# Neighbour aggregation by seven block products, with an earlier start of some group steps, in a graph and GRU layer

## The chip, the core and the metric

The kernel runs on one core of a Trainium2 chip. The metric is the device time in microseconds (us) of one execution; the time of a kernel is the median over its executions. Five engines work in parallel on the core: TensorE (PE in the profile; its weight loads are PEld), VectorE (DVE), ScalarE (ACT), GpSimd (POOL) and SyncE (SP, which here issues DMA transfers). Each takes its own instructions in order and waits on semaphores of the others.

## What is computed

There are B = 32 batches of N = 512 nodes with D = 256 features, all in float32. A layer norm and a relu come first; the layer has a convolution branch (a 1x1 convolution, then one of 17 taps), a neighbour aggregation and a GRU gate:

```python
h = jnp.maximum(_layernorm(x, axis=-1), 0.0)
# on h:
s = x @ w_se.T + b_se                                # 3 values per node
sq = jnp.sum(s * s, axis=-1)
dist = sq[:, :, None] + sq[:, None, :] - 2.0 * jnp.einsum('bnd,bmd->bnm', s, s)
A = jnp.exp(-dist) * mask                            # mask: a symmetric 0/1 adjacency
msg = jax.nn.relu(x @ w_msg.T + b_msg)
x_nmp = jnp.einsum('bnm,bmd->bnd', A, msg)           # the aggregation
x_in = jnp.concatenate([x_conv, x_nmp], axis=-1)
gi = x_in @ w_ih.T + b_ih
gh = x @ w_hh.T + b_hh
# r, z: sigmoids of the sums; n = tanh(gi_n + r * gh_n)
return (1.0 - z) * nn_ + z * x
```

The output is the input x plus the result of the layer.

## The kernel before

The batches are worked in two groups of 16 (GB). Each group has two stages, and one stage for all batches in pairs comes last.

`first_part(g)` makes the normalised rows (`statistics` L281, `normalise` L293), transposes them (`transpose_h` L307, hT, which is also written to memory), runs the 1x1 convolution (`conv1`) and takes the windows to a spectrum (`windows_to_freq`). The order in it is written by hand, in `manual_schedule`. Group one also builds the spectrum of the 17 taps there, and loads the weights of its first three spectrum products (`load_unit`, L911).

`nodes(g)` (L920) does two things side by side. One is the spectrum products (`product` L372, PSUM tile `py`, three products of two matmuls of 256 columns each): 36 units over the 16 batches in group one, so two or three in each iteration, and 40 units over the first 13 batches in group two, three each and four in the last, so that the last three iterations have none. POOL prepares a product (`both` L369 and L370, `wsum` L356), ACT and DVE take its result out (`y` L396 to L398). The other is the neighbour part, per batch:

- `load_h`, `by_chunks` (ACT copies, L422) bring hT in the order wanted.
- `message` (L425): eight matmuls of 259 columns into `pm` (256 of the message and 3 of s), the bias added by DVE (L438, L439), relu by ACT (L440).
- `features` (L442): five small DVE operations; `factors` (L452): transposes on PE into `psl`, `psr`, copied out by ACT.
- `affinity` (L464): four matmuls into `pd` (distances), the exponential on ACT into a tile `e` (L474), the transposed adjacency by DVE (`at`, L476), and the product of both by DVE (L477): the tile `A`.
- `aggregate` (L480): two times four matmuls of 128x128 by 512 columns into `pn` (L485), copied by ACT to `nmp` (L487), which `save_nmp` writes to memory.

The loop (L937 to L960) is staggered: iteration i makes the factors and affinity of batch i+1, the messages and features of batch i+2 (`begin(i + 2)`), and the aggregation of batch i, with products between. A scheduler may move instructions in `nodes`; a float32 matmul is two records in the profile[...].

The last stage (L992) works with pairs of batches. Its gates are matrix products on 2x2 blocks by seven products each, whose sums POOL makes in advance (`sums` L566). Before the first gates, POOL's queue issues the loads of the first pair (`load_pair(0, nc.gpsimd)`, L536 to L547: `hp`, `yt`, `np`) and of the gate weights (`load_combined` L532, `sw`); `inverse` (L572, PSUM tile pc) turns the spectrum back.

## Time and profile before

| what | us |
|---|---|
| median of 12 executions | 1847.69 |
| lowest and highest of them | 1844.35, 1853.54 |
| the profiled execution | 1846.12 |
| its span in the profile | 1844.3 |
| PE busy in the span | 1822.1 |
| DVE busy | 1102.9 |
| ACT busy | 582.6 |
| POOL busy | 589.0 |

By the timeline, `first_part(0)` runs to 166, `nodes(0)` to about 452, `first_part(1)` to 577, `nodes(1)` to 878.4, and the gates from there to the end. In a profile line, an entry such as L485 is a line of the kernel, `pn<-A,msg` says what is written from what, x512 counts instructions, and after the bar come busy time, the mean of one in ns, and the idle time just before with what ended it. In the chain of waits every line is start, length, engine, tile, line and count, in order of time; a stretch in which only PE stands there is one in which nothing but PE's own work sets the end.

### The profile page before, as it was taken

To read this page: it belongs to the slowest core of one execution; us is meant where nothing else is said; L and a number is where in the kernel's file an instruction comes from. 1 tells how busy PE (TensorE), PEld (TensorE's weight loads), DVE (VectorE), ACT (ScalarE), POOL (GpSimd) and SP (SyncE) were. 2 spreads that over 40 slices of the span, in tenths; PEclk is the share of its full clock that TensorE was granted. 3 is DMA by queue.
4 is the path that set the end of the run, shared out by engine and by line. 5 is a ranking of instruction groups with operands and counts; after the bars stand their busy time and mean duration, and the time that the engine had idled before them with its cause. 6 is when DMAs were issued, how large, how long until landed. Compare 5 with 4: busy or idle time off the path is not lost.

```text
span 1844.3 us, 20105 instructions
## 1 busy us (share of the span) xinstructions
PE 1822.1 (99%) x6610; PEld 1086.8 (59%) x6610; DVE 1102.9 (60%) x2221; ACT 582.6 (32%) x1082; POOL 589.0 (32%) x572
## 2 busy tenths in 40 slices
PE   9999999999999999999999999999999999999998
PEld 6777666666898676675545554555455544555443
DVE  7775655554885555545266456655666466645666
ACT  3545443432345334333222221222122221222121
POOL 3331333334432344445321323133222323133221
PEclk9999999999999999999999999999999999999999
DMA  9999898775578987777422443234422442244412
GB/s 230 301 277 240 238 253 240 192 208 182 187 245 207 245 246 234 219 205 258 116 86 36 118 120 107 57 77 120 120 83 38 120 120 91 48 101 120 112 25 52
DMA packets 307452, 289.26 MB, mean 157 GB/s; under 512 B 148028, under 2 KB 237148, under 8 KB 306964
## 3 DMA queue, kind: packets, MB, share of 16 engines
q1 hardware_dynamic: 281300, 224.22, 46.1%
q10 hardware_dynamic: 19024, 38.68, 5.8%
q0 software_dynamic: 7024, 25.07, 4.9%
q8 instruction: 53, 0.87, 0.2%
q14 instruction: 51, 0.42, 0.1%
HBM read 191.50 MB, written 96.40 MB: 156 GB/s over the span
## 4 chain that ended last, share of the span: by engine, by line
PE 90%; DVE 3%; issue 2%; POOL 2%; DMA 2%; ACT 1%; SPq 0%; POOLq 0%; ACTq 0%; DVEq 0%
PE pg L592 29%; PE pn L592 14%; PE pn L485 12%; PE py L390 11%; PE pm L436 6%; PE pc L580 5%; PE pc L325 3%; PE px L340 3%; PE pw L256 2%; PE pd L471 2%; PE phT L312 1%; DMA w<-in_w_ihT_dram 1%; PE psr L460 1%; DVE xn L304 1%; DVE stats L285 1%
## 5 line engine op out<-in xcount | busy, mean ns | idle before, releaser
L485 PE MATMUL pn<-A,msg 128*128 128x512 f32 x512 | 225.0, 592 | 0.0
L592 PE MATMUL pg<-hp,sw 128*128 128x512 f32 x434 | 221.8, 593 | 0.7 <-DVE rz L611 0.5
L592 PE MATMUL pg<-cp,sw 128*128 128x512 f32 x434 | 221.6, 592 | 0.0
L592 PE MATMUL pg<-np,sw 128*128 128x512 f32 x434 | 221.6, 592 | 0.0
L570 POOL TENSOR_TENSOR hp<-hp 128x512 f32<-128x512 f32 x64 | 81.0, 1276 | 412.2 <-DMA hp<-hd 293.2
L369 POOL TENSOR_TENSOR both<-xf 128x256 f32<-128x256 f32 x78 | 60.7, 778 | 325.1 <-PE py L390 293.9
L485 PEld LDWEIGHTS pn<-A,msg 128*128 128x128 f32 x512 | 97.1, 190 | 110.6 <-issue 107.7
L570 POOL TENSOR_TENSOR cp<-cp 128x512 f32<-128x512 f32 x64 | 80.5, 1269 | 233.5 <-ACT cp L586 232.2
L390 PE MATMUL py<-wt,both 128*128 128x256 f32 x624 | 150.4, 384 | 0.7 <-issue 0.7
L607 ACT ACTIVATE rz<-rz,brz 128x512 f32<-128x512 f32 x93 | 67.2, 724 | 260.0 <-DVE rz L611 260.0
L397 DVE TENSOR_TENSOR y<-y,py 128x256 f32<-128x256 f32 x78 | 31.9, 409 | 190.7 <-ACT y L396 190.7
L592 PEld LDWEIGHTS pg<-hp,sw 128*128 128x128 f32 x434 | 82.2, 190 | 104.8 <-issue 98.1
L592 PEld LDWEIGHTS pg<-np,sw 128*128 128x128 f32 x434 | 82.5, 190 | 103.8 <-issue 103.8
L592 PEld LDWEIGHTS pg<-cp,sw 128*128 128x128 f32 x434 | 82.5, 190 | 103.8 <-issue 103.8
L390 PEld LDWEIGHTS py<-wt,both 128*128 128x128 f32 x624 | 114.1, 190 | 42.9 <-issue 29.1
L477 DVE TENSOR_TENSOR A<-e,at 128x512 f32<-128x512 f32 x128 | 111.9, 912 | 36.5 <-ACT e L474 36.2
L356 POOL TENSOR_TENSOR wsum<-wt 128x512 f32<-128x512 f32 x78 | 108.2, 1388 | 49.6 <-DMA wt<-wd 39.2
L730 ACT ACTIVATE nt<-nt,vech 128x512 f32<-128x512 f32 x64 | 46.4, 725 | 235.4 <-DVE nt L729 235.4
L325 PE MATMUL pc<-w,hT 128*128 128x256 f32 x512 | 118.2, 384 | 2.0 <-DVE hT L313 2.0
L436 PE MATMUL pm<-wmsg,hq 128*128 128x259 f32 x512 | 117.6, 382 | 1.0 <-ACT hq L422 1.0
L592 PE MATMUL pn<-np,sw 128*128 128x512 f32 x224 | 114.4, 592 | 0.0
L592 PE MATMUL pn<-cp,sw 128*128 128x512 f32 x224 | 114.4, 592 | 0.0
(145 smaller groups left out, 2956.7 us busy)
## 6 DMA issues: line engine op xcount, KB each, us to landing
wt<-wd SPq DMA_DIRECT2D x160, 256.0 KB, 4.2
adj<-in_adj_dram SPq DMA_DIRECT2D x128, 256.0 KB, 5.7
wd<-wst SPq DMA_DIRECT2D x64, 320.0 KB, 5.0
yd<-y ACTq DMA_DIRECT2D x80, 256.0 KB, 4.2
yt<-yd SPq DMA_DIRECT2D x30, 640.0 KB, 7.4
hd<-hT SPq DMA_DIRECT2D x32, 512.0 KB, 4.3
nd<-nmp ACTq DMA_DIRECT2D x32, 512.0 KB, 4.2
xb<-in_x_dram SPq DMA_DIRECT2D x128, 128.0 KB, 3.8
```

Of the source, the lines that this page charges most:

```text
L325: nc.tensor.matmul(p[:, j, :], HT[b][:, ic, c * P : (c + 1) * P], w1[:, ic, :], start=(ic == 0), stop=(ic == DC - 1))
L340: nc.tensor.matmul(p[:, j * 2 * L : (j + 1) * 2 * L], H1[b][:, c0 + j, ic * P : (ic + 1) * P], fwd, start=True, stop=True)
L356: nc.gpsimd.tensor_tensor(t, WT[g, u][:, 0], WT[g, u][:, 1], op=ALU.add)
L369: nc.gpsimd.tensor_tensor(both[:, 0], re, im, op=ALU.add)
L390: nc.tensor.matmul(dst, v[:, ic, :], w[:, ic, :], start=(ic == 0), stop=(ic == DC - 1))
L436: nc.tensor.matmul(p[:, : D + NS], hq[:, ic, c * P : (c + 1) * P], wmsg[:, ic, :], start=(ic == 0), stop=(ic == DC - 1))
L477: nc.vector.tensor_mul(A[b][:, mc, :], e, at)
L485: nc.tensor.matmul(p, MSG[b][:, mc, dc * P : (dc + 1) * P], A[b][:, mc, :], start=(mc == 0), stop=(mc == NC - 1))
L570: nc.gpsimd.tensor_tensor(t[:, dst, :], t[:, a, :], t[:, b, :], op=sub)
L580: nc.tensor.matmul(bk[:, t0:t1], YT[p][j][:, c, oc * P : (oc + 1) * P], back[:, n : n + t1 - t0], start=(c == 0), stop=(c == len(spans) - ...
L592: nc.tensor.matmul(bk[:, t], sw[:, k, q, o, :], terms[k][q][:, t], start=(first and i == 0), stop=(i == len(ks) - 1), skip_group_check=True)
L607: nc.scalar.activation(rz[:, g, j, :], src, AF.Sigmoid, bias=brz[:, g : g + 1], scale=1.0)
```

## The change

The aggregation is computed by seven products on 2x2 blocks instead of eight matmuls of 512 columns. Per batch, message blocks are summed by DVE (`message_sums`, four operations of 128x256), affinity blocks by POOL (`affinity_sums`, four of 128x512), and seven block products of two matmuls of 256 columns each go into three PSUM tiles, b1 to b3, of which the same half is used. The results come out by two ACT copies and five DVE adds. `aggregate` is now a generator with three parts, two blocks, then three, then two; the affinity of the next batch lies between the first and the second part, a product between the second and the third. The exponential is written straight into `A`, the tile `e` is gone, and `at` and `sr` have one buffer instead of two.

Besides: at the start of each group the order is by hand, and the two halves of the second batch's message lie before and after the first factors; in group two the statistics of the third batch come ahead of the second's normalise, and its normalise ahead of the second's transposes; hT of batch 0 is half made on ACT; `load_h` is one batch further ahead and comes behind `begin`; and the weights of the first three products are loaded behind `first_part(0)`.

```diff
@@ transpose_h
-            nc.vector.tensor_scalar(HT[b][:, dc, :], p, 0.0, None, op0=ALU.max)
+            if b == 0 and dc > 0:
+                nc.scalar.activation(HT[b][:, dc, :], p, AF.Relu)
+            else:
+                nc.vector.tensor_scalar(HT[b][:, dc, :], p, 0.0, None, op0=ALU.max)
@@ message
-    def message(b):
+    def message(b, halves=range(2)):
...
-        for c0 in range(0, NC, h):
+        for c0 in (h * k for k in halves):
@@ factors
-        t = SR[b] = pools["nodes"].tile([P, N], FP, tag="sr", name=f"sr_{b}", bufs=2)
+        t = SR[b] = pools["nodes"].tile([P, N], FP, tag="sr", name=f"sr_{b}", bufs=1)
@@ affinity
-            e = pools["nodes"].tile([P, N], FP, tag="e", name=f"e_{b}_{mc}", bufs=2)
-            nc.scalar.activation(e, pd[mc], AF.Exp)
-            at = pools["nodes"].tile([P, N], FP, tag="at", name=f"at_{b}_{mc}", bufs=2)
+            nc.scalar.activation(A[b][:, mc, :], pd[mc], AF.Exp)
+            at = pools["nodes"].tile([P, N], FP, tag="at", name=f"at_{b}_{mc}", bufs=1)
             nc.vector.transpose(at.rearrange("p (j k) -> p j k", k=32), ADJ[b][:, :, 32 * mc : 32 * (mc + 1)])
-            nc.vector.tensor_mul(A[b][:, mc, :], e, at)
+            nc.vector.tensor_mul(A[b][:, mc, :], A[b][:, mc, :], at)
@@ new
+    def message_sums(b):
+        m = MSG[b].rearrange("p (k c) (i d) -> p i k c d", k=2, i=DC)
+        (a11, a12), (a21, a22) = (m[:, 0, 0], m[:, 0, 1]), (m[:, 1, 0], m[:, 1, 1])
+        t = SM[b] = pools["nodes"].tile([P, 3, H2, P], FP, tag="sm", name=f"sm_{b}", bufs=1)
+        s1, s2, s4 = (t[:, k] for k in range(3))
+        nc.vector.tensor_add(s1, a21, a22)
+        nc.vector.tensor_sub(s2, s1, a11)
+        nc.vector.tensor_sub(a21, a11, a21)
+        nc.vector.tensor_sub(s4, a12, s2)
+
+    def affinity_sums(b):
+        m = A[b].rearrange("p (k c) (j n) -> p k j c n", k=2, j=2)
+        (b11, b12), (b21, b22) = (m[:, 0, 0], m[:, 0, 1]), (m[:, 1, 0], m[:, 1, 1])
+        t = TA[b] = pools["nodes"].tile([P, 3, H2, N // 2], FP, tag="ta", name=f"ta_{b}", bufs=1)
+        t1, t2, t4 = (t[:, k] for k in range(3))
+        sub = ALU.subtract
+        nc.gpsimd.tensor_tensor(t1, b12, b11, op=sub)
+        nc.gpsimd.tensor_tensor(t2, b22, t1, op=sub)
+        nc.gpsimd.tensor_tensor(b12, b22, b12, op=sub)
+        nc.gpsimd.tensor_tensor(t4, b21, t2, op=sub)
@@ aggregate
-        for dc in range(DC):
-            p = bank(f"pn_{b}_{dc}")
-            for mc in range(NC):
-                nc.tensor.matmul(p, MSG[b][:, mc, dc * P : (dc + 1) * P], A[b][:, mc, :],
-                                 start=(mc == 0), stop=(mc == NC - 1))
-            nc.scalar.copy(NMP[b][:, dc, :], p)
+        def into(bk, w, v, first):
+            for c in range(H2):
+                nc.tensor.matmul(bk[:, lo], w[:, c], v[:, c], start=(first and c == 0), stop=(c == H2 - 1), skip_group_check=True)
+
+        b1, b2, b3 = (bank(f"pn{k}_{b}") for k in range(3))
+
+        p1, u2, u3 = out[:, 1, lo], out[:, 0, hi], out[:, 1, hi]
+        into(b1, m[:, 0, 0], a[:, 0, 0], True)
+        nc.scalar.copy(p1, b1[:, lo])
+        into(b2, s2, t2, True)
+        nc.vector.tensor_add(u2, p1, b2[:, lo])
+        yield
+        into(b1, m[:, 0, 1], a[:, 1, 0], False)
+        nc.scalar.copy(out[:, 0, lo], b1[:, lo])
+        into(b2, m[:, 1, 0], a[:, 0, 1], False)
+        nc.vector.tensor_add(u3, p1, b2[:, lo])
+        into(b3, s1, t1, True)
+        nc.vector.tensor_add(out[:, 1, hi], u3, b3[:, lo])
+        yield
+        into(b2, m[:, 1, 1], t4, False)
+        nc.vector.tensor_add(out[:, 1, lo], p1, b2[:, lo])
+        into(b3, s4, a[:, 1, 1], False)
+        nc.vector.tensor_add(out[:, 0, hi], u2, b3[:, lo])
+        yield
@@ first_part
         statistics(b0 + 1)
+        if g > 0:
+            statistics(b0 + 2)
         normalise(b0 + 1, g > 0)
...
-                transpose_h(b + 1)
-                statistics(b + 2)
-                normalise(b + 2)
+                if g == 0:
+                    transpose_h(b + 1)
+                    statistics(b + 2)
+                    normalise(b + 2)
+                else:
+                    normalise(b + 2)
+                    transpose_h(b + 1)
@@ before nodes(0)
-                mine = spread(steps, b, GB - 1) if b < GB - 1 else [partial(load_unit, 0, u) for u in range(3)]
+                mine = spread(steps, b, GB - 1) if b < GB - 1 else []
...
+                for u in range(3):
+                    load_unit(0, u)
@@ nodes
-            begin(0)
-            factors(todo[0])
-            begin(1)
+            with tc.manual_schedule():
+                begin(0)
+                message(todo[1], [0])
+                factors(todo[0])
+                message(todo[1], [1])
+                features(todo[1])
             affinity(todo[0])
...
-                if i + 2 < GB and todo[i + 2] not in HT:
-                    load_h(todo[i + 2])
                 if more:
                     load_adj(todo[i + 1])
                     factors(todo[i + 1])
+                parts = aggregate(b)
+                message_sums(b)
+                affinity_sums(b)
                 for u in mine[:1]:
                     product(pools["pw"], g, u, xf)
                 begin(i + 2)
+                if i + 3 < GB:
+                    load_h(todo[i + 3])
+                next(parts)
                 if more:
                     affinity(todo[i + 1])
+                next(parts)
                 for u in mine[1:2]:
                     product(pools["pw"], g, u, xf)
-                aggregate(b)
+                next(parts)
                 save_nmp(b)
```

## The prediction

> **What bounds the kernel now.** I read the page first: the share of each engine, then the slices. The first line below says that TensorE (PE) is busy for 99% of the span, so an edit that shortens PE's work pays in full until another engine becomes later, and one that makes PE wait costs in full.
>
> ```profile
> PE 1822.1 (99%) x6610; PEld 1086.8 (59%) x6610; DVE 1102.9 (60%) x2221; ACT 582.6 (32%) x1082; POOL 589.0 (32%) x572
> ```
>
> Next the chain of waits in the two loops over batches. Columns are start, length and what. One iteration with two spectrum products (`py`) is a closed row of PE pieces, without "issue" and without another engine:
>
> ```profile
> 338.73 2.59 PE py L390 x12
> 341.32 3.51 PE pm L436 x16
> 344.83 1.07 PE pd L471 x8
> 345.90 2.79 PE py L390 x12
> 348.69 6.87 PE pn L485 x16
> 355.56 0.11 PE psl L455
> 355.67 0.44 PE psr L460 x4
> ```
>
> The view by windows gives busy time of PE, PEld, DVE, ACT, POOL over an iteration with two products and one with three:
>
> ```profile
> 338.73:356.10 17.37, 17.37 (x71) 11.35 (x70) 9.89 (x25) 7.04 (x16) 5.97 (x6) 1.00 0.81 214
> 707.72:727.67 19.95, 19.95 (x82) 13.63 (x82) 10.72 (x28) 7.40 (x16) 8.64 (x10) 1.00 0.76 225
> ```
>
> The reader is to see that PE has no gap, and that VectorE (DVE) has 7.5 us of room in the first and 9.2 us in the second. The prices come from the groups (total, mean ns):
>
> ```profile
> L485 PE MATMUL pn<-A,msg 128*128 128x512 f32 x512 | 225.0, 592 | 0.0
> L390 PE MATMUL py<-wt,both 128*128 128x256 f32 x624 | 150.4, 384 | 0.7 <-issue 0.7
> L477 DVE TENSOR_TENSOR A<-e,at 128x512 f32<-128x512 f32 x128 | 111.9, 912 | 36.5 <-ACT e L474 36.2
> L476 DVE STREAM_TRANSPOSE at<-adj 128x512 f32<-128x512 f32 x128 | 83.2, 686 | 0.1
> L570 POOL TENSOR_TENSOR cp<-cp 128x512 f32<-128x512 f32 x64 | 80.5, 1269 | 233.5 <-ACT cp L586 232.2
> ```
>
> One number is odd: the multiply on line 477 means 912 ns, yet some take 650. Two narrow windows of the timeline show why. In the first, a multiply of 0.69 is running when POOL's weight sum begins; in the second, the next multiply has joined:
>
> ```profile
> 332.12 0.69 DVE L477 TENSOR_TENSOR A<-e,at 128x512 f32<-128x512 f32 x1
> 332.21 1.72 POOL L356 TENSOR_TENSOR wsum<-wt 128x512 f32<-128x512 f32 x1
> ```
>
> ```profile
> 332.12 2.36 DVE L477 TENSOR_TENSOR A<-e,at 128x512 f32<-128x512 f32 x2
> ```
>
> The weight sum takes 1.72 instead of the 1.27 of line 570's adds: it waits out the multiply. The second multiply takes 2.36 - 0.69 = 1.67: it waits until POOL has ended. They take turns, one whole instruction each. Adds with a PSUM operand (0.42 for 256 columns) and transposes are not stretched.
>
> Last the end of group two, in the chain and on POOL's queue:
>
> ```profile
> 854.60 7.08 PE pn L485 x16
> ...
> 864.47 13.93 PE pn L485 x32
> 878.40 5.65 PE pc L580 x40
> ```
>
> ```profile
> 850.03 0.76 POOL L542 DMA_DIRECT2D hp<-hd  x1 [10.23 <-PE psr L460]
> ...
> 859.76 1.63 POOL L534 DMA_DIRECT2D sw<-ws  x3
> ```
>
> The last product ends at 849.48; aggregations end 28.9 later, and the gates start at 884.05, 34.6 later. POOL, idle then, issues the loads of the first pair of the next stage from 850.03, so that they land under the aggregations.
>
> **What the Trainium skill says.** "SBUF — State Buffer", section "SBUF: two separate sides": a DVE operation with two SBUF inputs and a GpSimd operation that reads SBUF share a port pair under an exclusive lock; who starts first holds it for the whole instruction and the other blocks. The trace agrees: 0.45 us lost by POOL, then 1 us by DVE, above. "GPSIMD Engine Reference", section 3.1: a float32 `tensor_tensor` takes 1.96 times as long on GpSimd as on DVE; here 1.27 against 0.65, agreed. "TensorE: Matmul & The Clock Gate", section on LDWEIGHTS: a load's cost follows its columns, so halving the moving columns doesn't halve it. The trace has 190 ns a load beside 2.59/12 = 216 ns for a 256-column record, so loads stay hidden, narrowly.
>
> **The change part by part.**
>
> (a) Products on TensorE. A float32 matmul is two records. Before: 16 records of 512 columns, 6.87 us. After: seven products of two matmuls of 256 columns, 28 records x 0.216 = 6.05 us. Saved 0.82 a batch, 26 us over 32 batches if PE stays the bound. PE then needs 16.5 for two products and 19.1 for three.
>
> (b) VectorE per batch: four message sums at 0.45 (both inputs SBUF) and five adds from PSUM at 0.42, that is 3.9 us. ScalarE (ACT): two copies of 256 columns (about 0.37 each, as line 396) for two of 0.59, nothing. POOL: four affinity sums at 1.27, 5.1 us.
>
> (c) Where they fall. The built order of each engine shows POOL's affinity sums of the next batch after the last `both` and `wsum` of the iteration, and DVE's message sums of the same batch after the last two PSUM adds; both become free in the middle of the iteration. Count from the start of the first PSUM add (`u2`). DVE: 0.42, then four multiplies, three transposes, two PSUM adds, in all 5.9; the first transpose of the batch after 0.69; two `y` adds and two PSUM adds 1.7: message sums start at 8.3. POOL: the second product ends on PE at 4.9 (0.42 + two blocks of 0.86 + 2.79), then `both` twice and `wsum`, 2.8: affinity sums start at 7.8. So they meet, and by the turns seen above the four message sums take about 6.3 instead of 1.8. Then two `y` adds 0.84, four `st`/`msg` pairs 2.3, features 0.9, and the ACT relu (0.63) with the copy of p1 (0.4), which must end before the next `u2`, partly beside the features: 18.5 from `u2` to `u2`. Against 17.37 before, +1.1 in each of the ten two-product iterations of group one. An iteration with three products has 19.1 of PE and one more pair of `y` on DVE, about equal; I take 19.4, -0.5. Group one has three of them: 11 - 1.5, and +0.8 for its two last, irregular iterations: **+10**. Group two has twelve: **-6**. The bounds of an iteration with two products are 16.5 (DVE and POOL miss each other) and 19.5 (each of DVE's two multiplies beside `both` and `wsum` also waits).
>
> (d) Starts of the groups. Before the first aggregation nothing runs under the affinity's four exponentials, transposes and multiplies, and now POOL's sums follow: two sums, 2.5, before block two can go. In group one the order puts DVE's work for the first affinity after the adds and features of the second message, so the second affinity sum is ready some 8 to 9 after that message, with products for only about 3: PE waits 6 where it waits 2 to 3 now. **+4** (0 to +6). Group two interleaves these: **+3.5** (0 to +5). Half the second message ahead of the factors hides about 1 us of the features' wait at each start, counted in these.
>
> (e) End of group two. Iterations 13 to 15 have no product. Each batch there is a chain: distances, four multiplies with transposes (5.9), four POOL sums (5.1, with turns 5.7), the last blocks. From the last product's end: the message and distances of the last two batches to about 7, multiplies to 12.8, sums to 19; the last distances wait behind block two at about 18, multiplies to 24, sums to 29.4, last blocks to 32 to 34. And POOL's queue holds the loads of the first pair behind those sums. Before they were issued from 850.03, 0.6 after the last product; now from 29.4 after it. `yt` lands 8.2 after its issue (its row in the DMA view) at 38.4, the inverse takes 5.65 to 44; three weight loads issued at about 34.5 land 10.7 later, at 45 to 46. Gates start at 45.5 instead of 34.6: **+11** (7 to 14).
>
> (f) Statistics and normalise earlier at group two's start take away a wait of PE of 3.34 on `xn` there: **-3** (0 to -3.4); the transpose takes over the place of the normalise, which is later for the third batch but has a whole batch to spare. The relu of batch 0 on ACT, the three weight loads moved to behind the first stage on SP's queue (needed only when the first product starts, 14 us later), and loading `hT` one batch earlier: **-0.5**, hidden under PE; if not, a load of 4.2 us late once. Buffers of `at` and `sr` cut to one: `at` is written and read by DVE in order, and `sr` is free after the distances, a whole iteration ahead, nothing.
>
> Sum: 10 - 6 + 4 + 3.5 + 11 - 3 - 0.5 = +19. On the span: 1844.3 + 19 = 1863; the profiled run is 1846.12, 1.8 more than its span, and the median 1847.69 is 1.6 above that run: 1847.7 + 19 = **1867**.
>
> **The rivals.** A difference under 0.2% (3.7 us) can't be told from none.
>
> 1. The sums miss each other (not slower). If POOL's sums and DVE's message sums don't meet, or DVE's slack before features takes it up, iterations run at PE's 16.5 and 19.2: -8 and -2 in group one, -8 in group two; starts +5, end +9, rest -3.5: -7, or 1841. For it: DVE's work without turns is 9.9 + 3.9, under 14, well below 16.5. It decides from the point where DVE's loop stays below 16.5, that is, where less than about 2 us of turns are lost. Against it: both queues are released by the same product.
>
> 2. DVE and POOL collide more: 19.5 with two products, 20.3 with three, 14 at the end: 21 + 6 + 8 + 14 - 3.5 = +45, 1893. For it: two of the four multiplies wait on POOL already now. Against: in the new order most multiplies precede `both`.
>
> 3. The change doesn't save on PE: with 190 ns of load beside 216, a block of two matmuls could stream at 0.25 a record, 28 x 0.25 = 7.0. Then three-product iterations gain nothing: 19 + 9 = +28, 1876. Against: `py` has the same shape, at 0.216.
>
> **How the numbers follow.** Forecast 0.60 (own range 1856 to 1880), rival one 0.18, two 0.15, three 0.07. Rival one's own spread puts 0.12 on faster, 0.05 on the same, 0.01 on slower; another 0.01 of the same comes from the forecast's edge. Low end 1845 leaves out about 0.12, high end 1893 some 0.08.
>
> **What would show it.** Aggregation records at 0.216; the DVE message sums at 1 to 1.7 instead of 0.45 and POOL's sums at 1.7, alternating; gaps of PE of 1 to 2 us ahead of the block that waits for `u2` in two-product iterations and none in three; the first `hp` load after the last affinity sum and gates 45 after the last product. Wrong would be message sums at 0.45 with iterations of 16.5, or loads of the first pair issued before the sums.

## The result and the profile after

The changed kernel takes 1908.03 us (median of 8, 1903.87 to 1913.62) beside 1847.93 for the kernel before on the same chip, a ratio of 1.0324, 95% interval 1.0307 to 1.0341: it is 60 us slower. One execution of each was profiled; that of the changed kernel has a span of 1906.3, 62.0 more than before.

The page of the changed kernel, busy time and share of the span by engine, then TensorE's clock in 40 slices:

```profile
PE 1836.7 (96%) x6994; PEld 1166.7 (61%) x6994; DVE 1304.0 (68%) x2508; ACT 562.3 (29%) x1083; POOL 760.9 (40%) x700
...
PEclk9999899999999899999999999999999999999999
```

TensorE is busy 14.6 us longer, although its work shrank, and idle for 69.6 us instead of 22.2, that is 47.4 more; the two make 62.0. VectorE has 201 us more and POOL 172. The two slices of the clock below 9 are new. A slice is 47.7 us, so they are 191 to 238 and 620 to 667: the starts of the two groups.

Where the time went is read from the start times of `psl`, the first operation of each batch's factors, before and after:

| stretch | before | after | change |
|---|---|---|---|
| to the first factors of group one | 170.8 | 169.8 | -1.0 |
| group one, next four iterations' factors | 57.8 | 78.9 | +21.1 |
| group one, the rest, to its last factors | 198.9 | 201.4 | +2.5 |
| to the first factors of group two | 154.2 | 156.8 | +2.7 |
| group two, next three | 45.1 | 58.1 | +12.9 |
| group two, to the last factors with a product ahead of them | 222.6 | 224.5 | +1.9 |
| from there to the first gate product | 34.6 | 50.4 | +15.8 |
| the gates | 960.4 | 966.5 | +6.1 |

So the two starts cost 34, the end and what it makes late in the gates 22, and the steady loops, which I had thought the main point, 4.4 together. The last 1.7 are in the two stretches ahead of the first factors.

TensorE in the timeline of the changed kernel, start of group two (start, length, what, count, and the idle time before it with what ended it):

```profile
617.35 0.59 PE L522 MATMUL pn<-A,msg 128*128 128x256 f32 x2
618.62 0.70 PE L522 MATMUL pn<-A,msg 128*128 128x256 f32 x2 [0.67 <-DVE A L483]
620.60 0.67 PE L522 MATMUL pn<-A,msg 128*128 128x256 f32 x2 [1.29 <-DVE A L483]
622.26 1.22 PE L522 MATMUL pn<-A,msg 128*128 128x256 f32 x2 [0.98 <-DVE A L483]
623.66 2.08 PE L522 MATMUL pn<-ta,sm 128*128 128x256 f32 x4 [0.18 <-POOL ta L508]
625.67 2.09 PE L478 MATMUL pd<-sr,sl 9*128 9x512 f32 x8
...
645.51 2.08 PE L394 MATMUL py<-wsum,xf 128*128 128x256 f32 x4 [4.76 <-POOL wsum L360]
```

Three things are to be seen. The first blocks wait three times for the multiplies of the first affinity. From 622 on, four records take 2.08 where the same take 1.03 elsewhere, and eight `pd` records 2.09 instead of 1.14: TensorE runs at half its clock, which the profile gives as 0.50 of full speed from 621.3 to 631.5. And 20 us later it waits 4.76 us for a weight sum on POOL. The timeline of POOL there says why that came late:

```profile
635.20 1.27 POOL L507 TENSOR_TENSOR ta<-A 128x512 f32<-128x512 f32 x1
637.69 0.73 POOL L373 TENSOR_TENSOR both<-xf 128x256 f32<-128x256 f32 x1 [1.22 <-PE py L394]
639.11 1.27 POOL L508 TENSOR_TENSOR ta<-A,ta 128x512 f32<-128x512 f32 x1 [0.69 <-DVE A L483]
640.33 1.45 POOL L509 TENSOR_TENSOR A<-A 128x512 f32<-128x512 f32 x1
641.75 1.44 POOL L510 TENSOR_TENSOR ta<-A,ta 128x512 f32<-128x512 f32 x1
643.14 0.90 POOL L374 TENSOR_TENSOR both<-xf 128x256 f32<-128x256 f32 x1
644.01 1.45 POOL L360 TENSOR_TENSOR wsum<-wt 128x512 f32<-128x512 f32 x1
```

The weight sum stands behind the affinity sums in POOL's queue, and the second of them waits for a multiply of the second affinity, which is late because its distances stood behind the first blocks on TensorE. One lateness goes through three queues. Group one has a wait of 4.0 for a weight sum as well, at 226; there the four sums ahead of it run without a gap from 223.1, so that it is their place in the queue, and no late multiply, that holds it up.

The groups of the changed kernel by form (busy, mean ns of one) have the message sums, which I had priced at 450 alone, and POOL's sums, priced at 1270:

```profile
L498 DVE TENSOR_TENSOR msg<-msg 128x256 f32<-128x256 f32 x32 | 46.5, 1454 | 0.0
L509 POOL TENSOR_TENSOR A<-A 128x512 f32<-128x512 f32 x32 | 46.0, 1439 | 0.0
...
L499 DVE TENSOR_TENSOR sm<-msg,sm 128x256 f32<-128x256 f32 x32 | 42.7, 1333 | 0.0
L497 DVE TENSOR_TENSOR sm<-sm,msg 128x256 f32<-128x256 f32 x32 | 41.9, 1309 | 1.0
```

The message sums take turns with POOL's sums, as forecast; the first of the four (L496) has a mean of 645. In a steady three-product iteration (20.17 us, 0.2 more than before) the saving of the blocks is lost elsewhere; TensorE at the last two blocks:

```profile
677.17 1.89 PE L394 MATMUL py<-wt,both 128*128 128x256 f32 x8
678.90 1.03 PE L394 MATMUL py<-wsum,xf 128*128 128x256 f32 x4
680.14 1.13 PE L522 MATMUL pn<-ta,msg 128*128 128x256 f32 x4 [0.21 <-DVE nmp L535]
681.55 1.13 PE L522 MATMUL pn<-A,sm 128*128 128x256 f32 x4 [0.28 <-DVE nmp L537]
682.52 1.89 PE L394 MATMUL py<-wt,both 128*128 128x256 f32 x8
```

From the end of the product (about 679.8) to the next one 2.8 us pass for eight records that need 1.7 in step: each of the two blocks goes into a PSUM tile from which VectorE has yet to add, so about 1 us is lost where the shorter blocks save 0.8.

The end of group two, on POOL:

```profile
903.33 1.28 POOL L507 TENSOR_TENSOR ta<-A 128x512 f32<-128x512 f32 x1 [13.82 <-PE pn L522]
...
916.31 1.27 POOL L507 TENSOR_TENSOR ta<-A 128x512 f32<-128x512 f32 x1 [7.48 <-PE pn L522]
...
920.28 1.44 POOL L510 TENSOR_TENSOR ta<-A,ta 128x512 f32<-128x512 f32 x1
921.68 0.76 POOL L598 DMA_DIRECT2D hp<-hd  x1
...
926.42 1.63 POOL L590 DMA_DIRECT2D sw<-ws  x3
```

The loads of the first pair start at 921.68, right behind the last affinity sum and 32 us after the last product (889.6), where they started 0.6 us after it before. The two waits of 13.82 and 7.48 on `pn` are read as those for the one buffer of the sums, `ta`: the sums of a batch overwrite what the last blocks of the batch before still read. A second buffer was not tried. The blocks that hold the buffer are late themselves, since from 880 to 1000 TensorE waits four times, 5.9 us in all, for VectorE's add of u3 (L535).

### The profile page after: what moved, and what is told of

The parts are those of the page before. It is cut to its first block, busy times and chain, and to the rows that moved or that the text cites. A ratio compares the mean times of both kernels' runs of the same rounds, so it can differ in the third digit from the quotient of the medians.

```text
span 1906.3 us, 21332 instructions
## 1 busy us (share of the span) xinstructions
PE 1836.7 (96%) x6994; PEld 1166.7 (61%) x6994; DVE 1304.0 (68%) x2508; ACT 562.3 (29%) x1083; POOL 760.9 (40%) x700
## 4 chain that ended last, share of the span: by engine, by line
PE 56%; DVE 5%; issue 3%; POOL 2%; DMA 1%; ACT 0%; POOLq 0%; DVEq 0%
PE pg L648 28%; PE pn L648 14%; PE pc L636 4%; PE py L394 3%; PE pm L441 2%; PE pn L522 2%; DVE A L483 2%; DVE at L482 2%; PE pd L478 1%; DMA np<-nd 1%; DMA sw<-ws 1%; ACT A L480 0%; PE psr L467 0%; DVE nmp L537 0%; POOL np L626 0%
## 5 line engine op out<-in xcount | busy, mean ns | idle before, releaser
L648 PE MATMUL pg<-hp,sw 128*128 128x512 f32 x434 | 222.6, 594 | 1.9 <-DMA sw<-ws 1.1
L626 POOL TENSOR_TENSOR cp<-cp 128x512 f32<-128x512 f32 x64 | 80.5, 1269 | 223.1 <-ACT cp L642 221.7
L483 DVE TENSOR_TENSOR A<-A,at 128x512 f32<-128x512 f32 x128 | 101.7, 795 | 28.8 <-ACT A L480 21.3
L522 PE MATMUL pn<-A,msg 128*128 128x256 f32 x384 | 105.5, 409 | 12.2 <-DVE A L483 6.7
L648 PE MATMUL pn<-hp,sw 128*128 128x512 f32 x224 | 114.4, 592 | 0.0
L441 PEld LDWEIGHTS pm<-wmsg,hq 128*128 128x128 f32 x512 | 98.5, 193 | 16.0 <-ACT hq L426 0.2
```

What stands on the lines that cost most here:

```text
L441: nc.tensor.matmul(p[:, : D + NS], hq[:, ic, c * P : (c + 1) * P], wmsg[:, ic, :], start=(ic == 0), stop=(ic == DC - 1))
L483: nc.vector.tensor_mul(A[b][:, mc, :], A[b][:, mc, :], at)
L522: nc.tensor.matmul(bk[:, lo], w[:, c], v[:, c], start=(first and c == 0), stop=(c == H2 - 1), skip_group_check=True)
L626: nc.gpsimd.tensor_tensor(t[:, dst, :], t[:, a, :], t[:, b, :], op=sub)
L648: nc.tensor.matmul(bk[:, t], sw[:, k, q, o, :], terms[k][q][:, t], start=(first and i == 0), stop=(i == len(ks) - 1), skip_group_check=True)
```

## The experiments

Ratios are to the kernel before on the same chip, with 95% intervals; the changed kernel stands at 1.0324. Differences in us are between the medians of the times; by the ratios they come out up to 3 us larger. The diffs are shortened to what each edit comes to.

**First: is it the order of the first iteration?** In the first iteration of each group the three parts of the aggregation come last:

```diff
-                next(parts)
+                if i > 0: next(parts)
                 if more:
                     affinity(todo[i + 1])
-                next(parts)
+                if i > 0: next(parts)
                 for u in mine[1:2]:
                     product(pools["pw"], g, u, xf)
-                next(parts)
+                for _ in range(1 if i > 0 else 3): next(parts)
```

> The changed kernel, but in the first iteration of each group all three parts of the aggregation come after the next batch's distances and the second product (where the aggregation stood before the change); all other iterations as changed. In the trace of the changed kernel the first three iterations of group one lost 20 us and of group two 13.5 us against before. Theory A (order at the start: TensorE reaches the first blocks before the first affinity and its sums exist, so the next distances, the next affinity, its POOL sums and the weight sum queued behind them on POOL all come late, and the clock halves after the gap): 18 to 28 us faster than the changed kernel, 1880 to 1890. Theory B (the amount of work, four message sums and four affinity sums more per batch with nothing prepared ahead, is what is late, wherever the aggregation stands): at most 6 us faster, 1902 or more.

Measured 1907.0, ratio 1.0311 (1.0286 to 1.0335): no gain. In group one the first iteration is 6 us shorter (20.8), and the next two more than take it back (26.5 and 27.5 instead of 21.2 and 25.0). The waits of TensorE from 160 to 260 us in this run (waiting line, releaser, total, times, longest):

```profile
PE py L394 <- POOL wsum L360: 7.0, 1, 7.0
PE pn L522 <- DVE A L483: 3.8, 4, 1.8
```

The weight sum behind affinity sums is waited for longer than in the changed kernel (4.0). Theory A is refuted: the position of the first aggregation alone isn't the cause.

**Loads of the first pair on SP's queue.**

```diff
-        load_pair(0, nc.gpsimd)
+        load_pair(0)
...
-            nc.gpsimd.dma_start(sw[:, k, q0:q1], WS[k][:, q0:q1])
+            nc.sync.dma_start(sw[:, k, q0:q1], WS[k][:, q0:q1])
```

> The changed kernel, with the loads of the first pair and of the gate weights issued on SP's queue instead of POOL's. Between the last spectrum product and the first gate product the changed kernel takes 50.4 us, the one before 34.6, and 6 us more are lost in the first gates. Theory A (the loads stand behind the last affinity sums in POOL's queue): the loads land under the last aggregations, gates start about 40 us after the last product, 12 to 18 us faster, 1890 to 1896. Theory B (the last aggregation itself, which ends 37.1 us after the last product instead of 28.9, is the limit, and the loads wait for memory or for the last result anyway): at most 5 us faster, 1903 or more.

Measured 1895.71, ratio 1.0244 (1.0224 to 1.0263): 12 us less than the changed kernel, theory A at the low end. TensorE at the end of group two in this run:

```profile
927.79 1.03 PE L522 MATMUL pn<-A,sm 128*128 128x256 f32 x4
928.65 5.81 PE L636 MATMUL pc<-back,yt 128*128 128x136 f32 x40
934.30 1.02 PE L648 MATMUL pg<-hp,sw 128*128 128x512 f32 x2
```

No idle time is left between the last block, the inverse and the gates. The first gate product comes 46.1 us after the last product, 4.3 earlier than in the changed kernel and not at the 40 expected, and the gates take 960.6, as before the change. What remains, 11.5 us, is that the last block itself ends late.

**All edits but the seven products.** The aggregation of before in its old place, no sums:

```diff
-                parts = aggregate(b)
-                message_sums(b)
-                affinity_sums(b)
...
+                aggregate_four(b)   # as aggregate before the change
                 save_nmp(b)
```

> The changed kernel with the aggregation of before (eight matmuls of 512 columns, in its old place, no message or affinity sums), and all other edits kept: statistics and normalise of group two's third batch, half messages around the first factors, one buffer for at and sr, exponential straight into A, later and earlier loads. Theory A (all the loss belongs to the seven products): 1843 to 1850, level with the kernel before. Theory B (the other edits, the single transposed buffer and the new start order above all, cost by themselves): 1856 or more. In group two's first stage 2.65 us were lost between the last factors of group one and the first of group two; if that belongs to the moved statistics it is still there, if to the late end of group one it is gone.

Measured 1844.96, ratio 0.9972 (0.9962 to 0.9981), theory A. The whole loss belongs to the seven products and their sums. The stretch to the first factors of group two, 156.8 after the change and 154.2 before, is 151.5 here: the moved statistics do give 2.6 us, and the changed kernel loses 5.3 in this stretch. Of these, 2.5 lie ahead of the first transposes of group two, where the last batches of group one end late; 2.8 lie behind them, where the clock is halved once more, from 573.5 to 576.9. The gain of the medians is 4.5 us. The two profiled spans, 1844.5 and 1844.3, don't show it: that of the kernel before is of an execution 3.4 us below the median here, that of this run of one 1.3 above its own. Between these two profiles the 2.6 are lost again by 2.9 in the first four iterations of group one. So 2.9 of the 21.1 there come without any seven products. In group two a wait of 1.8 us for a product's weights stands in the third iteration, but the first two are shorter, and the start is level with that of before (44.9).

**The aggregation late in every iteration.** As the first diff, with the condition always false.

> The changed kernel with the three parts of the aggregation one behind the other after the second product in every iteration, as the aggregation stood before the change. Theory A (the split is needed in the steady iterations, since each further block into a PSUM tile waits for VectorE's add from it, and is harmful only at the start): starts gain some 25 us, 29 steady iterations lose 0.5 to 1.5 each, 1895 to 1920. Theory B (the early part of the aggregation is what makes everything late): 1880 or less.

Measured 2012.47, ratio 1.0874 (1.0850 to 1.0899), far beyond both theories. Behind the starts iterations take 20 to 27 us; in group one from 240 on TensorE waits ten times for the add of u2:

```profile
PE pn L522 <- DVE nmp L530: 35.4, 10, 4.6
```

With the parts in a row, the add stands behind the multiplies of the next affinity on VectorE. The split is needed, and the early part was not what hurt.

**Aggregation of before in the first two iterations of each group.**

```diff
+                seven = i > 1
```

> The changed kernel with the aggregation of before (eight matmuls, no sums) in the first two iterations of each group, seven products from the third on. Moving the whole aggregation of the first iteration late (the earlier run) shifted the loss by an iteration: TensorE then waited 7.0 us for a weight sum that stood in POOL's queue behind affinity sums, themselves waiting for multiplies. Theory A (the loss of 20 and 13.5 us belongs to the first affinities, made without lead; once the loop runs in step the sums fit): most of it goes, 1874 to 1884. Theory B (the changeover comes at whatever iteration the sums first stand in POOL's queue, since weight sums and affinity sums have to find their order there): the loss moves to the third and fourth iteration, 1898 or more.

Measured 1886.0, ratio 1.0201 (1.0183 to 1.0220): 22 us less. Group two's start is level with the kernel before (its stretch of three iterations takes 45.0), so there theory A holds. Group one still loses 8.3 against before in the iteration in which the sums first stand in POOL's queue; without any seven products 3.0 of these are there too (21.6 against 18.6), and the other 5.3 are as theory B said. POOL in that stretch:

```profile
207.13 1.26 POOL L507 TENSOR_TENSOR ta<-A 128x512 f32<-128x512 f32 x1 [9.43 <-DVE A L483]
208.35 1.71 POOL L360 TENSOR_TENSOR wsum<-wt 128x512 f32<-128x512 f32 x1
```

POOL is idle for 9.43 us for a multiply, with a weight sum behind it that TensorE needs: one wait of 5.3 us.

**Affinity sums on VectorE.** `nc.vector` for `nc.gpsimd` in the four lines of `affinity_sums`.

> The changed kernel with the four affinity sums on VectorE instead of POOL. No lock is left between the two kinds of sums, and POOL's queue holds only both and wsum (and the loads of the first pair). Theory A (POOL's queue and the lock are what costs): message sums back at 0.45 each, affinity sums 0.65 each, no wait for a weight sum of more than 1 us at the starts, loads of the first pair issued early; VectorE's own 2.6 us more fit in three-product iterations: 15 to 30 us faster than the changed kernel, 1878 to 1893. Theory B (VectorE is the engine that is late, and POOL's queue only passes its lateness on): two-product iterations grow by 1 to 2 us, starts stay, 1900 to 1925.

Measured 1893.49, ratio 1.0236 (1.0217 to 1.0255), 15 us less. The message sums mean 509 to 1066 ns (645 to 1454 in the changed kernel), and no wait for a weight sum above 0.4 is left at the starts. But two-product iterations grow to 17.2 to 19.5 and three-product ones to 20.7: both theories in part. POOL's queue costs at the starts and at the end; in the loop VectorE doesn't take the sums without loss.

**The last part behind the third product.**

```diff
-                next(parts)
-                save_nmp(b)
                 for u in mine[2:]:
                     product(pools["pw"], g, u, xf)
+                next(parts)
+                save_nmp(b)
```

> The changed kernel with the last part of the aggregation (two blocks, and the write of the result) behind the third product of an iteration instead of in front of it; two-product iterations as changed. In the trace of the changed kernel a steady three-product iteration takes 20.17, 0.2 more than before, although its blocks need 0.8 less: the last two blocks wait for VectorE's adds from their PSUM tiles (gaps of 0.21 and 0.28 and longer first records). Theory A (that wait eats the gain): three-product iterations fall to 19.1 to 19.4, 12 us over fifteen of them, 1893 to 1899. Theory B (VectorE's loop is the limit in these too, the wait only moves): within 3 us of the changed kernel.

Measured 1905.55, ratio 1.0306 (1.0288 to 1.0325), not told apart from the changed kernel. Some iterations take 22 and 23, and TensorE now waits for the copy of the first block (4.0 us in five waits from 700 to 890). The wait is moved rather than removed, theory B. But single iterations reach 19.14, as theory A says. One of them, by windows (length, busy time of PE, PEld, DVE, ACT, POOL, then the clock):

```profile
848.22:867.36 19.14, 19.14 (x94) 15.87 (x93) 17.04 (x37) 7.00 (x16) 14.28 (x14) 1.00 0.74 216
```

**Seven products only where products cover them,** in the third to the thirteenth batch of group two, with the last part behind the third product (`seven = g > 0 and 1 < i < last`).

> Seven products only in the third to the thirteenth batch of group two, the last part behind the third product; all other batches have the aggregation of before. Theory A (starts and the end are where the seven products lose, covered three-product iterations are where they gain 0.6 to 0.8 each, eleven of them): 1836 to 1841, faster than both. Theory B (no gain in the covered iterations, and a changeover loss at the third): 1845 to 1858.

Measured 1844.41, ratio 0.9970 (0.9959 to 0.9981), the same as without any seven products (0.9972): no gain in the covered iterations, which vary between 19.1 and 24.5. The slow one, by windows (columns as above):

```profile
731.00:733.50 2.50, 2.50 (x13) 1.91 (x11) 2.46 (x5) 0.00 (x0) 2.50 (x3) 1.00 1.07 345
733.50:736.80 3.30, 2.09 (x9) 0.98 (x8) 3.30 (x14) 2.42 (x6) 3.00 (x4) 0.91 0.76 230
736.80:740.50 3.70, 3.62 (x9) 2.90 (x10) 3.29 (x6) 2.36 (x6) 0.00 (x0) 0.50 0.41 142
```

For 3.3 us TensorE does eight distance records and waits 1.29 us for the copy of the first block, which stands behind late message adds; then it runs 3.7 us and more at half clock.

**Weight sums ahead, first try.** In the first three iterations of each group, the order of the program by hand, with the first two products prepared ahead of the affinity sums.

> The changed kernel, with the first three iterations of each group in the order of the program and, in these, the preparation of the first two products (both and wsum on POOL) ahead of the affinity sums in POOL's queue. All aggregations by seven products. Theory A (at the start the loss is mainly a weight sum standing in POOL's queue behind affinity sums that wait for VectorE's multiplies: 4.0 and 4.8 us in the changed kernel, 5.3 and 7.0 in two of the runs so far, each with some 4 us more at half clock after the gap): no wait for a weight sum of over 1 us at the starts, 10 to 20 us faster than the changed kernel, 1888 to 1898. Theory B (the first multiplies and sums are late anyway, and TensorE then waits for them in their place): at most 6 us faster, 1902 or more.

Measured 1918.59, ratio 1.0383 (1.0368 to 1.0397). The waits for weight sums are gone, but the order by hand put ScalarE's copies of hT late, which TensorE now waits for (from 160 to 240 us):

```profile
PE pm L441 <- ACT hq L426: 8.7, 2, 6.9
PE pn L522 <- POOL ta L508: 3.6, 1, 3.6
```

So it doesn't show how much the weight sums cost; another way follows below.

**Aggregation of before for the last three batches of group two** (`seven = g == 0 or i < last`).

> The changed kernel with the aggregation of before for the last three batches of group two, which have no products beside them; nothing is left in POOL's queue ahead of the loads of the first pair. Theory A (the end costs what the trace shows, 15.8 us up to the first gate product and 6 in the first gates): 20 to 24 us faster than the changed kernel, 1884 to 1888. Theory B (only the loads' place counts, which moving them to SP's queue has already given back, 12 us): 1894 to 1898.

Measured 1889.74, ratio 1.0221 (1.0206 to 1.0237), 18 to 19 us less, nearer to theory A. The first gate product comes 36.3 us after the last product of the spectrum, counted as in the table; it was 50.4. The gates take 960.7.

**Both of the last two edits together.**

> The two last changes together: weight sums ahead in the first three iterations of each group, and the aggregation of before for the last three batches of group two; seven products in the other 29 batches. If the two losses are independent, this is the changed kernel less the sum of both gains. Theory A: 1865 to 1877, and the rest above the kernel before is what the first affinities and their sums still cost, plus 0.2 us in each steady iteration. Theory B (the losses overlap or move): 1880 or more.

Measured 1896.46, ratio 1.0266 (1.0247 to 1.0285): about the sum of the first edit's loss of 11 and the second's gain of 18, so theory B by number, and only because the first of the two edits loses.

**Message sums on POOL as well,** with seven products only in the third to the thirteenth batch of group two.

> The earlier run with seven products only in the third to the thirteenth batch of group two (last part behind the third product), and now the message sums on POOL as well as the affinity sums. VectorE loses four instructions that took 1.3 to 1.5 us each beside POOL's sums, 0.45 alone; POOL gets 2.9 us more. Theory A (VectorE, held up by the lock, is what made those iterations take 20 and more where 19.14 were seen at best): iterations of 19.1 to 19.3, 1836 to 1841. Theory B (POOL becomes late, 16.6 of 19.1 us busy, and weight sums come late): 1845 or more.

Measured 1856.54, ratio 1.0041 (1.0028 to 1.0054), theory B: 12 us more than with these sums on VectorE (0.9970). POOL's own message sums take 0.73 to 0.79, but the block that needs s2 waits for them (690 to 860 us):

```profile
PE pn L522 <- POOL sm L497: 9.2, 5, 2.6
```

**Weight sums ahead, second try.** No order by hand; in the first three iterations POOL issues the affinity sums behind the second product's weight sum:

```diff
-                affinity_sums(b)
+                if i < 3:
+                    for u in mine[:2]:
+                        if u > 0 and (g, u) not in BOTH:
+                            prepare(pools["pw"], g, u, xf)
+                    with tc.issue_after(LASTSUM[0].ins):   # the last weight sum
+                        affinity_sums(b)
+                else:
+                    affinity_sums(b)
```

> The changed kernel with one edge more: in the first three iterations of each group POOL issues the affinity sums only behind the weight sum of the iteration's second product; no order by hand, so that the copies on ScalarE stay where they were (in the earlier run they came late and hid the answer). Theory A (the weight sum behind waiting affinity sums is a cause of the loss at the starts): its waits of 4.0 and 4.8 us on TensorE and the half clock behind them go, 8 to 16 us faster than the changed kernel, 1892 to 1900. Theory B (what is late at the starts is the affinity with its sums as such; with the weight sums first, TensorE waits for the second affinity sum instead): 1903 to 1920, with waits for ta in place of waits for wsum.

Measured 1902.71, ratio 1.0285 (1.0265 to 1.0305), 5 to 7 us less than the changed kernel, between the theories. The waits of 4.0 and 4.8 are gone; in group one another of the same size stands in their place, for the copy of the first block:

```profile
216.75 1.47 PE L522 MATMUL pn<-A,msg 128*128 128x256 f32 x4 [4.51 <-ACT nmp L528]
```

The weight sum is a link of the chain, and not its origin. What the origin is, beyond the late first affinities, no run isolates.

**A product between the parts,** seven products in group two's third to thirteenth batch.

> Seven products only in the third to the thirteenth batch of group two, as before, but now one product between the first and the second part of the aggregation and one between the second and the third. In the earlier run of this kind TensorE still waited for the copy of the first block (0.5 to 1.3 us) where the second part followed the distances at once; the best iterations took 19.14. Theory A (with 3.7 us of TensorE work behind the first part and 2.6 behind the second, no block waits): iterations of 19.1 to 19.3 throughout, group two gains 7 to 9 us, 1836 to 1841. Theory B (VectorE, with its message sums at 1.3 to 1.5 us, needs about 20 us an iteration whatever TensorE's order): 1843 to 1848.

Measured 1850.0, ratio 1.0007 (0.9998 to 1.0017), and its iterations are even, at 20.52. TensorE's waits from 600 to 860:

```profile
PE pn L522 <- DVE nmp L535: 11.2, 10, 1.2
```

There is one wait of 1.1 to 1.2 us for the add of u3 in each iteration. One iteration by windows:

```profile
728.10:748.62 20.52, 19.41 (x94) 15.83 (x93) 17.66 (x36) 6.85 (x15) 13.96 (x14) 1.00 0.76 215
```

VectorE is busy for 17.7 of 20.5 us and waits for ScalarE for 1.8 of the rest. In this order its round takes 20.5. That is no fixed need, since single iterations of 19.14 with the same work, one of which is shown above, leave TensorE no gap. Theory B, some 2 us above what it gave.

**TensorE kept busy in the first gaps.** Five extra matmuls ahead of the first block, two behind each matmul of the first PSUM tile, in the first iteration of each group. They also change the sums of that tile, so that the output of this kernel is not that of the layer.

```diff
+        def keep(bk, n):
+            for _ in range(n):
+                nc.tensor.matmul(bk[:, hi], ident, wmsg[:, 0, : N // 2], start=True, stop=True, skip_group_check=True)
```

> The changed kernel with 13 extra matmuls of 256 columns (5.6 us of TensorE at full clock) in the first iteration of each group, in the unused half of the first block's PSUM tile, where TensorE waits for the first affinity; the output does not use them. Theory A (the gaps there are what sets TensorE to half its clock): the blocks and distances behind them run at full clock (0.216 a record instead of 0.43), which saves 4 to 6 us in each group against at most 2 us spent; the trace shows it, the time falls by 3 to 8 us, 1900 to 1905. Theory B (the half clock comes from elsewhere, or follows later anyway): the records stay at 0.43, 1908 to 1914.

Measured 1904.22, ratio 1.0286 (1.0261 to 1.0311). The blocks and distances of group one in the changed kernel:

```profile
190.74 2.07 PE L522 MATMUL pn<-ta,sm 128*128 128x256 f32 x4 [0.19 <-POOL ta L508]
192.75 2.09 PE L478 MATMUL pd<-sr,sl 9*128 9x512 f32 x8
```

The same in the timeline of this run:

```profile
183.33 2.32 PE L528 MATMUL pn<-wmsg,ident 128*128 128x256 f32 x10
...
192.28 1.13 PE L522 MATMUL pn<-ta,sm 128*128 128x256 f32 x4 [0.71 <-POOL ta L508]
193.35 1.14 PE L478 MATMUL pd<-sr,sl 9*128 9x512 f32 x8
...
228.28 2.07 PE L394 MATMUL py<-wsum,xf 128*128 128x256 f32 x4 [3.95 <-POOL wsum L360]
```

They run at full clock; behind the gap of 3.95, which nothing fills, the clock is again half. The iteration is 1.1 us shorter in this profile, and 1.2 in group two, although 5.6 us of work (26 records of 0.216) were added to each. Theory A in the mechanism. In the time it isn't shown: the interval overlaps that of the changed kernel, the profiled execution is even 1.9 us longer than its, and the clock lost over the whole kernel, estimated as below, falls only from 22.7 to 20.1, since there are new stretches at half clock, at 285 and 466 among others.

**Loads back in their old places,** without seven products.

> The changed kernel with the aggregation of before, as in the earlier run, and also with the loads of hT and of the first three product weights in their places of before. What stays of the change: the statistics and normalise of group two's third batch, the half messages around the first factors, one relu of batch 0 on ScalarE, one buffer for at and sr, the exponential straight into A. In the earlier run two waits of TensorE for a product's weights, 1.3 and 1.8 us, stood at the starts, and the stretches there came 3.3 and 2.3 us later than before. Theory A (the moved loads bring these waits): no such wait, 1841 to 1845, faster than the kernel before by 3 us or more. Theory B (the waits come from the earlier start of the group itself): 1845 to 1848.

Measured 1848.3, ratio 0.9992 (0.9981 to 1.0003), theory B at its upper edge. The wait of 1.8 us for a product's weights is still there in group two, so the moved loads don't bring it; that of 1.3 in group one is gone, and one of 2.7 of the distances stands there instead. The version without seven products and with all other edits, 0.9972, is faster than both kernels, by 0.3%; only the one with seven products in eleven batches, 0.9970, is level with it.

## Why the prediction was wrong

The direction was right, the size a third: +19 us forecast, 62 in the profile, and 1908 is above even the high end of 1893. Of the 43 us between them, 26.5 belong to the starts (d), 10.9 to the end (e), 5.2 to the stretches ahead of each group's first factors, (f) with the end of group one, and 0.4 to the loops (c). By its own parts:

(a) Blocks on TensorE: right. A 256-column record takes 0.216 in step, 28 make 6.05.

(b) and (c) The turns of VectorE and POOL: right as a mechanism. VectorE's message sums mean 0.65 to 1.45 and POOL's 1.27 to 1.44. The term was mis-sized both ways: a two-product iteration takes 17.1 to 18.5, in the mean some 0.3 over the 17.37 of before, where I took 18.5; a three-product one takes 20.17, where I took 19.4. Instead of +10 and -6 the loops gave +2.5 and +1.9; that the sum, +4, is met by 4.4 is luck. POOL's sums are not at the 1.7 that I had named as a sign, and no gap of 1 to 2 us stands ahead of a block that waits for u2: from 249 to 450 the blocks wait for the copy of the first one (three times, the longest 1.3) and for u3 and the add behind it (0.4 at most). In the three-product iterations I compared only the sums of work. I overlooked that a second block into a PSUM tile waits until VectorE has added the first; two such waits, with slower records behind them, make up the loss of about 1 us shown above.

(d) The starts: this is the step that failed, "PE waits 6 where it waits 2 to 3 now. +4", and +3.5 for group two. Measured +21.1 and +12.9. I priced one wait for the first affinity sums and stopped there. In its place the runs show a chain, in full in group two: the blocks wait, the next distances stand behind them on TensorE, the next multiplies and affinity sums come late, a weight sum behind these on POOL is waited for, 4.0 and 4.8 us, and each gap is followed by work at half clock. Aggregation of before in two iterations takes 22 us of it away; moving one aggregation only moves the wait, and putting the weight sums first gives 5 to 7. I had named what is queued behind POOL's sums at the end of group two, the loads, but not at the start. The other edits have 2.9 of the 21.1, by the profile of the run without seven products, and one wait of 1.2 us of the distances for a message add (at 212) fits a PSUM tile that wasn't yet free: the blocks now take three of these tiles where the aggregation took two, and whether that costs more was not tested.

The half clock was no term of the sum at all. From the windows of 2 us between 100 and 1000, TensorE's busy time times what is missing from the clock gives an estimate of the loss, 22.7 us after the change and 1.7 before. The Trainium skill has it, "TensorE: Matmul & The Clock Gate", Part 1: TensorE falls to half its clock after an idle window of about 3.4 us and returns after as long a busy one. This case agrees with the factor of two (2.08 for 1.03) and with the cause, by the run that fills the gaps. It differs in two points. The stretch need not be idle throughout: gaps of 0.67 and 1.29 in a row were enough here. And the half clock then lasted 10.2 us, although TensorE was busy without a gap over 0.2 for the last 9 of them.

(e) The end of group two: right in mechanism, +11 forecast, +15.8 measured up to the gates. The last sums end 32 us after the last product where I had 29.4. Missed are the waits for the one buffer of the sums, and 6.1 us behind the first gate product, where the rest of the gate weights comes late by the same queue. Of these 22 us, 10 go when the loads are on SP (4.3 ahead of the gates and 5.9 in them), and 11.5 are the late last block. In the time, loads on SP give 12 back, the aggregation of before there 18.

(f) The earlier statistics: right. They give 2.6 by themselves; in the changed kernel they are outweighed by 5.3 in the same stretch, for which (c) had +0.8. The -0.5 for the other small edits is not seen: the run without seven products loses 2.9 at the start of group one.

Rival one, where the sums miss each other, and rival three, where the blocks save nothing, are refuted by the lengths of the sums and of the records. Rival two, more collisions at 1893, was closest in time and not in cause; its 20.3 for three products is near the 20.17 measured, but two-product iterations are far from its 19.5.

That group one still loses 5.3 us by the sums when they begin in the third iteration, and group two nothing, is shown as a queue on POOL; why the scheduler's order is worse in group one stays open.

## What to carry to other kernels

In a loop that runs in step, a longer side chain may cost almost nothing (4.4 us here), and the same chain can cost much more at the start and the end (56), where nothing runs ahead: price these by following each late result through every queue in which something stands behind it, until a queue with slack is reached. A saving on a full engine is only had if the engine that empties its results has time for more of them: here TensorE waits for the adds of seven small results about as long as its shorter work had saved. And a gap on TensorE, or several short ones in a row, can cost more than its length, since the work behind the gaps of 4 to 5 us here ran at half clock. A single wait of 1.2 us in each iteration did not do this (the run with a product between the parts: clock 1.00 in the iteration shown).

## What the hardware showed unexpectedly

The half clock doesn't need an idle stretch, only one with little work, and it can outlast the gaps. Windows of the changed kernel at the start of group two, the first just ahead of the fall of the clock, the other three those at half clock (columns as above):

```profile
617.87:621.28 3.41, 1.44 (x5) 0.59 (x4) 3.35 (x7) 0.83 (x2) 1.27 (x1) 1.00 0.16 62
621.28:624.69 3.41, 2.25 (x5) 1.35 (x6) 1.20 (x7) 0.55 (x2) 2.35 (x2) 0.50 0.69 149
624.69:628.10 3.41, 3.41 (x12) 1.26 (x11) 0.42 (x1) 0.32 (x1) 1.36 (x2) 0.50 1.24 188
628.10:631.52 3.42, 3.42 (x9) 2.70 (x9) 1.05 (x3) 2.77 (x6) 0.00 (x0) 0.50 0.79 280
```

TensorE is busy for 1.44 of 3.41 us ahead of the fall, with no gap above 1.29. In the third window it is fully busy, and the clock still doesn't return; two of its 3.4 us are distances, which use nine of the 128 rows, and the fourth has none of them. Group one has the like at 191.2 to 194.6 and 194.6 to 198.0. Whether matmuls of few rows count for less is not shown, since no run separates it.

And work can cost less than waiting: 5.6 us of unused matmuls in such gaps made the first iteration of group one 1.1 us shorter, that of group two 1.2, though the kernel as a whole gained nothing clear of noise.
